# A four-layer graph network on one Trainium2 core: a lighter opening quarter of the scored sums, loads spread along it, and the first weights at the head of ScalarE's queue

## The chip, the cores and the metric

The kernel runs on one core of a Trainium2 chip. The metric is device time in microseconds (us), the lower the better. Times are medians of repeated executions; a profile is one further execution, recorded by the hardware profiler.

## What is computed

A batch of 16 graphs with 1024 nodes and 256 features passes four layers over one adjacency matrix `adj` (1024 x 1024, few of its entries not zero). Cut to what matters:

```python
# layer 0: every edge (u, v) has a score from both ends
pre_u = h @ W1[:256];  pre_v = h @ W1[256:]
S   = sigmoid(relu(pre_u[:, :, None] + pre_v[:, None, :] + b1) @ W2 + b2)
a_t = einsum('buv,bud->bvd', S * adj, h)          # the scored sums
m_t = einsum('uv,bud->bvd', adj, h) * h           # needs no score
x   = beta1 * h + beta2 * (a_t @ Wa + ba) + beta3 * (m_t @ Wm + bm)
# layer 1
x = x + relu((adj @ x) @ W.T + b)
# layers 2 and 3, softmax attention with exp(adj) as a factor
f = x @ W1.T;  f1 = f @ W2 + b2
x = softmax(leaky_relu(f1[:, :, None] + f1[:, None, :]) + adj) @ f + bias2 + x
```

## The kernel before

Only the edges that exist are scored. For each of 8 tiles of 128 nodes the kernel lists up to 16 neighbours per node in slots, and nodes with more get extra tiles of four slots. Four batches are worked on together as a group, so there are four groups. One **score step** treats one slot of one tile for one group: GpSimd gathers 128 rows of 4 KB (`z<-v_d`, L692), VectorE adds the other end (L802) and applies relu and the weight (L804), ScalarE sums it in four pieces (L808), and later GpSimd scatters the finished scores into a dense array in DRAM (`dense_d<-gt`, L697), of which the matrix products read whole tiles. Such a step moves 512 KB with its gather and 2 KB with its scatter. There are 608 of them. They are a side stream: `Side.along` (L864) adds, for each microsecond that the main stream yields as its own estimate, `RATE` steps, so that the order in which instructions are recorded interleaves the two. A scheduling layer then writes one instruction order for each engine, and every engine runs its own in order.

The main stream has these stages.

- **Opening** (L373 to L379). `load_h` loads the features of the first four batches. Batch 0 comes in four pieces of 256 KB, alternately on the SP queue and ScalarE's queue. `load_w1` (three transfers of 256 KB: both halves of W1, then Wa) follows on ScalarE's queue. `with_beta2` (L158) scales Wa on VectorE. Then come batch 1 and the adjacency matrix `adj_sb` in eight transfers on SP. TensorE turns `h` and multiplies it with W1 and Wa, while VectorE searches each row of `adj_sb` for its neighbours (L433 to L439). A flag that these searches compute decides a branch, which every engine takes.
- **The part without scores** for all 16 batches, with the scores of group 0 and some of group 1 as side stream at `RATE[0]`. Its results go to `zb_d` in DRAM.
- **Per group `with_edges`** (L1053), the scored sums: four quarters `v` of 256 columns. In each quarter, eight tiles `ut` of the dense scores are loaded on SP (`gd`, 512 KB, `load_gd`, four buffers), rearranged by ScalarE (`gc`, L1061) and multiplied on TensorE into all eight PSUM banks. At the quarter's end VectorE adds each bank to the loaded `z` (L1084), which frees the bank. The `z` of four batches (1 MB each, from `zb_d`) are loaded by `load_z`. For group 0 alone, these four loads are issued from inside the first quarter, and so are the loads of the transposed adjacency over `adj_sb` (eight of 512 KB), with an exponential by ScalarE for each (L1051).
- **Per group `pair_layers`**, twice: layers 1 to 3 for two batches.

`paced(ins, back)` (L117) makes an instruction wait until a matmul that lies `back` matmuls behind the newest recorded one has run; `back` is 6 if not given. VectorE's first operation of every score step is paced too. A load that is paced holds up all that stands behind it in SP's order.

Of the kernel before, what the change touches and what calls it, by code (L numbers as in the profile page):

```python
# [15 lines left out]
P = 128  # L16

GB = 4
BUFS = 2
RATE = (0.26, 0.255)  # L20
SLOTS = 32
FIRST = 16
EXTRA = SLOTS - FIRST
# [14 lines left out]
def after(tc, ins, others, kind, why):  # L38
    dep = mybir.DependencyInfo(kind, mybir.DependencyReason.DATA)
    for o in others:  # L40
        tc.add_manual_dep(ins.ins, o.ins.name, dep, reason=why)
# [23 lines left out]
def gnn_stack_kernel(  # L65
# [27 lines left out]
    nc = tc.nc  # L93
# [13 lines left out]
    def bank():  # L107
        return psum[-1].tile([P, HN], F32, tag="bank", name="bank")
# [8 lines left out]
    def paced(ins, back=6):  # L117


        if recent:  # L120
            after(tc, ins, [recent[max(0, len(recent) - back)]], mybir.DependencyClass.Sync, "keeps pace")
        return ins

    def product(*args, **kw):
        recent.append(nc.tensor.matmul(*args, **kw))  # L125
        del recent[:-BACK]
        return recent[-1]
# [22 lines left out]
    def load_w1(pool, queue):  # L150

        w = pool.tile([P, DH, 3, D], F32, name="w1")
        for s, a in enumerate((g0_W1[:D], g0_W1[D:], g0_Wa)):
            queue.dma_start(w[:, :, s, :], a.rearrange("(c p) k -> p c k", p=P))
        return w

    def with_beta2(w):
        return nc.vector.tensor_scalar(w[:, :, 2, :], w[:, :, 2, :], beta2, None, ALU.mult)  # L158
# [108 lines left out]
        flat = dense[i][:DUMP].rearrange("(c p r) b -> c p (r b)", p=P, r=ZERO // GB)  # L267
        return [flat[c] for c in range(flat.shape[0])]

    def load_h(pool, b, pieces=1, other=nc.sync):  # L270
        h = pool.tile([P, NT, D], F32, tag="wide", name="h")
        n = NT // pieces
        for t in range(0, NT, n):
            queue = other if t // n % 2 else nc.sync
            queue.dma_start(h[:, t : t + n, :], x[b, t * P : (t + n) * P].rearrange("(t p) d -> p t d", p=P))
        return h

    def node_pairs(t):
# [2 lines left out]
    def load_kept(pools, b):  # L281
        h = load_h(pools[0], b)
        hT = node_pairs(pools[0].tile([P, DH * N], F32, tag="wide", name="hT"))
        nc.sync.dma_start(hT.rearrange("p h n -> p (h n)"), hT_d[b])
        return h, hT
# [74 lines left out]
    with ExitStack() as stack:  # L360
        prep = stack.enter_context(tc.tile_pool(name="prep", bufs=4))
        prep1 = stack.enter_context(tc.tile_pool(name="prep1", bufs=1))
        early = stack.enter_context(tc.tile_pool(name="early", bufs=8))
        psum_pool(stack, "psum", 8)

        def first_group():
            for b in range(GB):
# [2 lines left out]
                yield 2.4  # L370
                yield from edge_sides(prep, b, w1, hT)

        hs = [load_h(early, 0, pieces=4, other=nc.scalar)]  # L373
        w1 = load_w1(prep1, nc.scalar)
        with_beta2(w1)
        hs.append(load_h(early, 1))
        for t in range(NT):
            nc.sync.dma_start(adj_sb[:, t, :], adj_v[:, t, :])
        hs += [load_h(early, b) for b in range(2, GB)]  # L379
# [292 lines left out]
    with tc.If(listed > 0) as arm:  # L672
        with ExitStack() as stack:
# [206 lines left out]
            def load_gd(g, v, ut, **pace):  # L880
                view = dense[g % BUFS][:DUMP].rearrange("(t p v) b -> t p v b", p=P, v=N)
                gd = gd_pool.tile([P, QN, GB], F32, tag="gd", name="gd")
                ins = nc.sync.dma_start(gd, view[ut][:, v * QN : (v + 1) * QN, :])
                put[g].before(paced(ins, **pace))
                return gd
# [16 lines left out]
            z_loads = []  # L902

            with ExitStack() as first:
# [12 lines left out]
                def score_free():  # L917
                    yield from turn_adj(
                        lambda n: wide_z.tile([P, DH * N], F32, tag="wide", name="stage")
                    )  # L920
                    h, hT = next_up
                    for b in range(B):
                        if b == 1:
                            nat = load_naturals(stage)
                            w1 = load_w1(own1, nc.sync)
                        if b == 2:
                            paced(with_beta2(w1))
                        if b >= GB:
                            yield from edge_sides(st_pool, b, w1, hT)
                        if b == B - 1:  # L930
                            first_hw.extend(load_hw(i) for i in range(GB - 1))
                            first_gd.extend(load_gd(0, 0, ut) for ut in range(4))
                        mT = yield from messages(pools, h, hT)
                        now = hT

                        if b + 1 < GB:
                            h, hT = load_kept(pools, b + 1)
                        elif b + 1 < B:
                            h = load_h(pools[0], b + 1)
                            hT = turned(pools[0], h)  # L940
                            yield 2.4
                        yield from without_edges(pools, b, now, mT, wm)
                        if b == 1:
                            prepare(nat)
                            yield 3

                def with_zeros(main):
                    for n, us in enumerate(main):
                        if 7 < n < 40 or n > 40 and n % 3 == 0:
                            clear()  # L950
                        yield us

                side.along(with_zeros(score_free()), RATE[0])
                assert not zeros
# [9 lines left out]
            to_load, to_exp = list(range(NT)), []  # L964
# [85 lines left out]
            def exponential(jt):  # L1050
                paced(nc.scalar.activation(ea[:, jt, :], ea[:, jt, :], AF.Exp), 16)  # L1051

            def with_edges(g, hw, z):  # L1053

                for v in range(N // QN):
                    cols = slice(v * QN, (v + 1) * QN)
                    acc = [[bank() for _ in range(DH)] for _ in range(GB)]
                    for ut in range(NT):
                        gd = first_gd.pop(0) if first_gd else load_gd(g, v, ut, back=BACK)
                        gc = gc_pool.tile([P, GB, QN], F32, tag="gc", name="gc")  # L1060
                        paced(nc.scalar.activation(gc, gd.rearrange("p n i -> p i n"), AF.Copy), 16)  # L1061
                        for i in range(GB):
                            for eh in range(DH):
                                product(
                                    acc[i][eh][:, :QN], hw[i][:, ut, eh * P : (eh + 1) * P], gc[:, i, :],
                                    start=ut == 0, stop=ut == NT - 1,
                                )
                        if z_loads and ut > 1:
                            load, i = z_loads.pop(0)
                            paced(load(i))  # L1070
                        if (to_load or to_exp) and ut % 2 and not z_loads:
                            if v and to_exp:
                                exponential(to_exp.pop(0))
                            if to_load:
                                jt = to_load.pop(0)
                                paced(nc.sync.dma_start(ea[:, jt, :], adjT_d[jt]), 16)
                                to_exp.append(jt)
                        yield 3.4
                    if v == N // QN - 1:
                        while to_exp:  # L1080
                            exponential(to_exp.pop(0))
                    for i in range(GB):
                        for eh in range(DH):
                            nc.vector.scalar_tensor_tensor(  # L1084
                                z[i][:, eh, cols], acc[i][eh][:, :QN], zbias[:, eh : eh + 1], z[i][:, eh, cols],
                                ALU.add, ALU.add,
                            )
# [109 lines left out]
            def ahead(g):  # L1197
                if g < NGR:
                    loaded.append(([load_hw(g * GB + i) for i in range(GB)], load_z(g)))
                    for load, i in z_loads:  # L1200
                        load(i)
                    z_loads.clear()

            for g in range(NGR):
                hw, z = loaded.pop(0)
                while g not in finished:
                    next(side.steps)
                side.along(with_edges(g, hw, z), RATE[1])
                side.along(pair_layers(g * GB, z[:2], lambda: None), RATE[1])
                side.along(pair_layers(g * GB + 2, z[2:], lambda: ahead(g + 1)), RATE[1])  # L1210
            assert next(side.steps, "end") == "end"
            psum.pop()

    with arm.Else():
        with ExitStack() as stack:
# [88 lines left out]
            with tc.For_i(0, B, 1) as b:  # L1304
                h = load_h(wide, b)
# [36 lines left out]
```

## Time and profile before

| | us |
|---|---|
| median of three executions (3267.03, 3267.06, 3274.82) | 3267.06 |
| the profiled execution, its own time | 3256.96 |
| its span on the core | 3255.1 |
| TensorE busy in the span | 3157.5 (97%) |
| VectorE busy | 2342.4 (72%) |
| ScalarE busy | 1879.1 (58%) |
| GpSimd busy | 1665.6 (51%) |

The mean granted TensorE clock of the profiled execution is 0.992 of full speed. All positions in the text are microseconds from the start of its span. Engine names in the views: PE is TensorE's matmuls, PEld its weight loads, DVE is VectorE, ACT ScalarE, POOL GpSimd, SP SyncE; SPq, ACTq and POOLq are what these sequencers issue. A matmul of 32-bit values is recorded as two passes.

### The profile page before, as it was taken

Reading aid. Unit: us, or ns where it says so; the run is one execution under the profiler, and the core shown is the slowest. Engines: PE = TensorE matmul, PEld = TensorE weight load, DVE = VectorE, ACT = ScalarE, POOL = GpSimd, SP = SyncE. Lnnn points to the kernel's source line nnn. Section 1 sums busy time; section 2 is a strip of 40 time slices with the busy share of each in tenths; the row PEclk is TensorE's granted clock in tenths of the full one; section 3 lists DMA queues with packets and bytes.
Section 4 is the critical chain, followed back from the end, with each engine's and each line's share of the span. In section 5 each row is a group of like instructions: output and inputs, shape, how many; then the busy total and the mean of one; then the engine's idle time right before and its main releaser. Section 6 shows DMA issues by size and latency. Waiting matters only on the chain. (4 is left out here: it accounts for less than half of the span.)

```text
span 3255.1 us, 38756 instructions
## 1 busy us (share of the span) xinstructions
PE 3157.5 (97%) x12162; PEld 2206.3 (68%) x12162; DVE 2342.4 (72%) x3217; ACT 1879.1 (58%) x6316; POOL 1665.6 (51%) x1338
## 2 busy tenths in 40 slices
PE   8899999999997999999999999999999999999999
PEld 5444545545456678578776867778686788778688
DVE  7787767777774799789678979877898881035154
ACT  3245556655667766566886656688666555322132
POOL 1156887686764666657566666665676650000000
PEclk9999999999998999999999999999999999999999
DMA  8998888878798755656875575597656635210100
GB/s 304 327 325 299 281 281 273 273 212 269 242 327 311 219 162 163 203 154 204 292 230 174 154 221 151 183 297 229 180 150 210 186 105 167 84 35 14 55 1 27
DMA packets 268438, 648.91 MB, mean 199 GB/s; under 512 B 42864, under 2 KB 131952, under 8 KB 261056
## 3 DMA queue, kind: packets, MB, share of 16 engines
q0 software_dynamic: 116704, 350.04, 36.8%
q1 hardware_dynamic: 123536, 244.66, 21.8%
q10 hardware_dynamic: 27984, 51.65, 4.2%
q8 instruction: 97, 1.59, 0.2%
q14 instruction: 117, 0.96, 0.1%
HBM read 518.84 MB, written 127.39 MB: 199 GB/s over the span
## 5 line engine op out<-in xcount | busy, mean ns | idle before, releaser
L808 ACT ACTIVATE z<-z 128x256 f32<-128x256 f32 x2432 | 979.7, 406 | 707.3 <-DVE z L804 678.2
L802 DVE TENSOR_TENSOR z<-z,u 128x1024 f32<-128x1024 f32 x608 | 738.8, 1220 | 408.2 <-PE bank L125 276.2
L125 PE MATMUL bank<-feats,m 128*128 128x257 f32 x4096 | 922.1, 383 | 20.8 <-DVE m L1033 18.7
L692 POOL DMA_INDIRECT z<-v_d,slot_v x512 | 645.9, 1262 | 463.8 <-ACT z L808 227.7
L125 PEld LDWEIGHTS bank<-feats,m 128*128 128x128 f32 x4096 | 766.3, 191 | 148.6 <-DVE m L1033 28.6
L804 DVE SCALAR_TENSOR_TENSOR z<-z,w2r 128x1024 f32<-128x1024 f32 x608 | 737.3, 1219 | 8.5
L697 POOL DMA_INDIRECT dense_d<-gt,slot_at x512 | 639.2, 1249 | 197.9 <-issue 134.7
L125 PE MATMUL bank<-gc,hw 128*128 128x256 f32 x2048 | 455.6, 384 | 30.5 <-ACT gc L1061 27.7
L808 ACT ACTIVATION_READ_ACCUMULATOR z<-z 128x1 f32 x2432 | 461.2, 190 | 0.0
L125 PEld LDWEIGHTS bank<-gc,hw 128*128 128x128 f32 x2048 | 387.2, 191 | 98.2 <-ACT gc L1061 40.4
L1033 DVE SCALAR_TENSOR_TENSOR m<-rho,tau,adj_sb 128x512 f32<-128x512 f32 x512 | 374.0, 743 | 107.7 <-PE bank L125 105.1
L125 PE MATMUL bank<-adj_sb,h 128*128 128x512 f32 x1024 | 442.4, 592 | 2.2 <-ACT st L318 2.1
L125 PE MATMUL bank<-adjT_in,y 128*128 128x512 f32 x1024 | 441.3, 592 | 1.4 <-DMA adjT_in<-adjT_d 1.4
L125 PEld LDWEIGHTS bank<-adjT_in,y 128*128 128x128 f32 x1024 | 194.4, 190 | 243.6 <-issue 228.6
L125 PEld LDWEIGHTS bank<-adj_sb,h 128*128 128x128 f32 x1024 | 194.4, 190 | 242.2 <-issue 237.7
L125 PE MATMUL bank<-w,hT 128*128 128x512 f32 (+1 forms) x1024 | 335.8, 488 | 6.8 <-DMA w<-in_L_gnn_W_dram 6.5
L1061 ACT ACTIVATE gc<-gd 128x1024 f32<-128x1024 f32 x128 | 265.5, 2074 | 88.2 <-PE bank L125 60.0
L125 PEld LDWEIGHTS bank<-w,hT 128*128 128x128 f32 x1024 | 195.0, 191 | 150.6 <-issue 126.3
L125 PE MATMUL bank<-g_wT,z 128*128 128x257 f32 x1024 | 232.9, 382 | 0.2 <-ACT st L1171 0.2
L692 POOL DMA_INDIRECT z<-v_d,x_node x96 | 127.1, 1324 | 181.8 <-ACT z L808 118.0
L125 PEld LDWEIGHTS bank<-g_wT,z 128*128 128x128 f32 x1024 | 192.9, 191 | 30.9 <-issue 3.8
L1123 DVE TENSOR_TENSOR z<-z,r 128x512 f32<-128x512 f32 x64 | 42.5, 689 | 135.2 <-ACT r L1122 134.9
(150 smaller groups left out, 2183.4 us busy)
## 6 DMA issues: line engine op xcount, KB each, us to landing
gd<-dense_d SPq DMA_DIRECT2D x128, 512.0 KB, 5.0
dense_d<-zero ACTq DMA_DIRECT2D x64, 512.0 KB, 5.9
adjT_in<-adjT_d SPq DMA_DIRECT2D x128, 256.0 KB, 3.3
h<-in_x_dram SPq DMA_DIRECT2D x19, 1024.0 KB, 12.9
u_d<-st SPq DMA_DIRECT2D x64, 256.0 KB, 5.7
v_d<-st SPq DMA_DIRECT2D x64, 256.0 KB, 6.5
hw_d<-st SPq DMA_DIRECT2D x64, 256.0 KB, 6.5
u<-u_d POOLq DMA_DIRECT2D x32, 512.0 KB, 8.1
```

The source lines that it names most:

```text
L125: recent.append(nc.tensor.matmul(*args, **kw))
L692: return nc.gpsimd.indirect_dma_start(out=dst, out_offset=None, in_=src[:], in_offset=bass.IndirectOffsetOnAxis(ap=at, axis=0), **how,)
L697: return nc.gpsimd.indirect_dma_start(out=dst[:], out_offset=bass.IndirectOffsetOnAxis(ap=at, axis=0), in_=src, in_offset=None,)
L802: paced(nc.vector.tensor_tensor(z, z, u, ALU.add))
L804: nc.vector.scalar_tensor_tensor(zk, zk, 0.0, w2r[:, None, :].to_broadcast([P, GB, D]), ALU.max, ALU.mult)
L808: nc.scalar.activation(zk[:, c, :], zk[:, c, :], AF.Copy, accum_out=s[:, k, c : c + 1])
L1033: nc.vector.scalar_tensor_tensor(m, r[:, cols], ta[:, jt : jt + 1], ea[:, jt, cols], ALU.max, ALU.mult)
L1061: paced(nc.scalar.activation(gc, gd.rearrange("p n i -> p i n"), AF.Copy), 16)
L1123: nc.vector.tensor_tensor(z[i][:, eh, cols], z[i][:, eh, cols], r, ALU.add)
```

## The change

- `RATE[1]`, the side stream's rate in `with_edges` and `pair_layers`, goes from 0.255 to 0.258.
- Opening: `load_w1` is issued first on ScalarE's queue, and all four pieces of batch 0 stand on SP's queue, ahead of batch 1. `with_beta2` is recorded after the loads of batches 0 and 1.
- Group 0, first quarter: the four `z` loads are recorded at tiles 0, 2, 4 and 6 instead of 2, 3, 4 and 5, and each is paced 12 matmuls back instead of 6. The adjacency loads begin in the second quarter instead of the first, and their exponentials in the third instead of the second. The quarter's tiles yield 1 instead of 3.4, so that the side stream gets 8 x 1 x 0.258 = 2.1 steps there instead of 8 x 3.4 x 0.255 = 6.9.

```diff
-RATE = (0.26, 0.255)
+RATE = (0.26, 0.258)
...
-    def load_h(pool, b, pieces=1, other=nc.sync):
+    def load_h(pool, b, pieces=1):
...
-            queue = other if t // n % 2 else nc.sync
-            queue.dma_start(h[:, t : t + n, :], x[b, t * P : (t + n) * P].rearrange("(t p) d -> p t d", p=P))
+            nc.sync.dma_start(h[:, t : t + n, :], x[b, t * P : (t + n) * P].rearrange("(t p) d -> p t d", p=P))
...
-        hs = [load_h(early, 0, pieces=4, other=nc.scalar)]
         w1 = load_w1(prep1, nc.scalar)
+        hs = [load_h(early, b, pieces=1 if b else 4) for b in range(2)]
         with_beta2(w1)
-        hs.append(load_h(early, 1))
...
-                        if z_loads and ut > 1:
+                        if z_loads and ut % 2 == 0:
                             load, i = z_loads.pop(0)
-                            paced(load(i))
-                        if (to_load or to_exp) and ut % 2 and not z_loads:
-                            if v and to_exp:
+                            paced(load(i), 12)
+                        if (to_load or to_exp) and ut % 2 and v:
+                            if v > 1 and to_exp:
                                 exponential(to_exp.pop(0))
...
-                        yield 3.4
+                        yield 3.4 if g or v else 1
```

## The prediction

> **What bounds the kernel now.** I read the busy row first, then TensorE's waits, then the two places that the edits touch. The page's first line gives the engine that can set the time:
>
> ```profile
> PE 3157.5 (97%) x12162; PEld 2206.3 (68%) x12162; DVE 2342.4 (72%) x3217; ACT 1879.1 (58%) x6316; POOL 1665.6 (51%) x1338
> ```
>
> TensorE is busy 97% of 3255.1 us, so 97.6 us is all that removing waits can bring. The waits of TensorE, longest in sum first, say which:
>
> ```profile
> PE bank L125 <- ACT gc L1061: 27.7, 16, 15.5
> PE bank L125 <- DVE m L1033: 18.7, 20, 2.4
> ...
> PE bank L125 <- DMA w<-in_L_gnn_W_dram: 6.5, 1, 6.5
> ```
>
> Columns: total us, times, longest. The 15.5 us piece and the 6.5 us piece belong to the two places edited. The first, in the timeline around group 0's first quarter:
>
> ```profile
> 961.49 0.32 SPq L883 DMA_DIRECT2D gd<-dense_d  x1
> ...
> 964.94 0.32 SPq L883 DMA_DIRECT2D gd<-dense_d  x1
> 965.81 3.77 SPq L897 DMA_DIRECT2D z<-zb_d  x2
> ...
> 972.24 0.32 SPq L1076 DMA_DIRECT2D adj_sb<-adjT_d  x1
> ...
> 973.10 3.92 SPq L897 DMA_DIRECT2D z<-zb_d  x2
> ...
> 977.11 1.35 SPq L883 DMA_DIRECT2D gd<-dense_d  x3
> ...
> 992.25 4.15 ACT L1061 ACTIVATE gc<-gd 128x1024 f32<-128x1024 f32 x2 [14.01 <-DMA gd<-dense_d]
> ```
>
> Columns: start, duration, engine, line, operation. The score tiles six and seven are issued only at 977.11, behind four `z` loads of 1 MB and one adjacency load, and the first of them reaches ScalarE 15 us later. The quarter in stretches:
>
> ```profile
> core 0: us, PE busy (x) PEld busy (x) DVE busy (x) ACT busy (x) POOL busy (x), PEclk, DMA share, GB/s
> 957.40:994.30 36.90, 21.30 (x97) 17.88 (x95) 13.80 (x15) 20.89 (x55) 24.21 (x20) 0.83 1.01 373
> 994.30:1001.40 7.10, 7.08 (x23) 5.88 (x24) 3.16 (x4) 3.63 (x9) 0.00 (x0) 0.68 0.48 164
> 1001.40:1094.60 93.20, 88.44 (x395) 73.14 (x394) 63.81 (x76) 91.28 (x206) 56.17 (x44) 1.00 0.86 285
> 1558.10:1672.90 114.80, 111.78 (x511) 95.40 (x510) 81.12 (x95) 108.48 (x261) 67.06 (x60) 1.00 0.85 280
> ```
>
> Until 994.3 the DMA engines are full (1.01) at 373 GB/s: this quarter is bound by DMA. The last three quarters (third row) are bound by ScalarE, busy 91.28 of 93.2. The fourth row is all four quarters of group 1, 114.8 us, of which TensorE needs 32 x 3.56 = 114: its timeline has 96 passes in 21.41 us from 957.41, and a tile takes 16 of them.
>
> **First quarter: minus 14.** DMA queues in the trace moved from 957.4 to 994.3: SP's 9.15 MB, GpSimd's 4.6 MB. Afterwards SP still owes all four `z` and five score tiles by the quarter's end, but not the adjacency tile: 9.15 - 0.5 = 8.65 MB. GpSimd's part falls with the score steps. The rate says five steps fewer; the instruction order of the built program has ScalarE do 6 steps between the quarter's first and last tile instead of 9, so 3 to 5 gathers of 0.52 MB go: 1.9 to 3.0 MB are left. At 373 GB/s, 10.6 to 11.7 MB take 28.3 to 31.2 us, beside 28.5 us of TensorE (8 tiles x 3.56). The order matters as much as the sum. In the built program the SP queue now alternates: the first `z` waits for a matmul five before the quarter, the others for the 14th, 30th and 46th, and between them come tiles four to nine. Tile six follows two `z` instead of four and is issued about 969 instead of 977.11. In the old queue 1 MB landed in about 3.4 us; counted so, tile six lands near 975.5, tile seven near 981 and the last `z` near 986.7, against TensorE's wish for 977, 980 and 986. So I expect the quarter to last 30 us instead of 44.0: -14. The ends: -9, if GpSimd keeps its bytes and 13.25 MB take 35 us; -15.5, if nothing but TensorE's 28.5 is left.
>
> The trace's clock adds to this: 0.68 after the wait against 1.00 in a running stretch. The Trainium skill, "TensorE: Matmul & The Clock Gate", Part 1, says the array returns to full speed after about 3.4 us of work; an estimate from that page is 1.7 us lost, where the row gives 7.1 x 0.32 = 2.3 us. Both lie inside the 44.0, and nothing is added for them.
>
> **Last three quarters: minus 1.** All eight exponentials (1.05 us each) remain, moved by one quarter. ScalarE's work per quarter is 8 tiles x 2.08 = 16.6, plus 1.6 per step (four sums at 0.40) and 1.05 for each `u` or exponential. Before, by the old program's order: 16.6 + 6 x 1.6 + 4.2 = 30.4, then 33.3, then 29.9, together 93.6, which the measured 93.2 confirms. After: 28.4 (TensorE 28.5 with little slack: 29), 30.4, and up to its last tile 32.3, together 91.7. That is -1.5; I take -1, with -4 and +3 as ends, because waits between the engines are not in such sums. Adjacency loads move on SP from the first quarter into a stretch with a DMA share of 0.86: 1 MB more there at 285 GB/s, covered; uncovered 2.7 us, inside the +3.
>
> **Opening: minus 1.** What is shown:
>
> ```profile
> 14.56 3.75 PE L125 MATMUL bank<-w,hT 128*128 128x512 f32 x4 [6.54 <-DMA w<-in_L_gnn_W_dram]
> 18.05 0.49 DVE L158 TENSOR_SCALAR w<-w,beta 128x512 f32<-128x512 f32 x1 [18.05 <-DMA w<-in_L_gnn_Wa_dram]
> ...
> 18.63 1.22 DVE L433 TENSOR_SCALAR_CACHE_REDUCE left<-adj_sb 128x1024 f32<-128x1024 f32 x1
> ```
>
> W's first two transfers will be where batch 0's pieces on ScalarE's queue were, and those landed, by the trace's completion counts, at 4.56 and 6.00. The third and fourth pieces of `h` come later on SP, between 8 and 10.5 instead of 5.6 to 6.0, so the sixteen turns end later too, and the first product starts at 9.5 to 11.5 instead of 14.56. These 3 to 5 us are not on the path. From 18.63 to 95.06 VectorE has no gap at all, and TensorE's small products with `full` and `missed` wait for it:
>
> ```profile
> 94.91 0.15 DVE L471 SCALAR_TENSOR_TENSOR missed<-counts,missed 128x1 f32<-128x1 f32 x1
> ...
> 95.21 0.35 PE L473 MATMUL bank<-missed,ones 128*128 128x1 f32 x2
> 95.42 10.57 PE L125 MATMUL bank<-w,hT 128*128 128x512 f32 x32
> ```
>
> TensorE gets there just when VectorE is ready. Starting earlier, it waits 3 to 4 us here. Only an earlier start of VectorE counts, and that needs the first adjacency tile, which in the trace landed at 18.61, 0.07 after `with_beta2`. On each DMA engine the same 3.25 MB stand ahead of or in this tile, in whichever queue. The DMA engines have slack in the first 20 us (share 0.82), so it may come 3 us earlier; GpSimd's small transfers may also take the share that ScalarE's queue gives up and delay it 2 us. I take -1; ends -3 and +2.
>
> Here a rule speaks against the edit. The Trainium skill, "DMA: Bandwidth & Descriptors", Issuing engines are not separate DMA queues, says that transfers of all issuing engines interleave on the same 16 DMA engines, and that issuing from several saves issue time only. By it the opening is worth 0; by TensorE's wait alone it would be -6.5.
>
> **The rest: plus 1.** The steps saved come back in `pair_layers`: by the built order 112, 113 and 102 beside groups 0 to 2 instead of 111, 111 and 101. Each brings one gather on GpSimd's queue, two VectorE operations (2 x 1.22), four on ScalarE and a scatter. VectorE is busy 87.5% there, and TensorE idles 36.9 us beside 323 steps, 0.11 us a step: four steps cost 0.5 so, or 9.8 with all VectorE time exposed. I take +1. The scheduler also reorders small pieces (turns of `feats`, `top`, `val`) there; the waits that this shuffles are 1 to 2.4 us each, one 5.9, and I allow 6 either way.
>
> Sum: -14 - 1 - 1 + 1 = -15, from 3256.96 to 3242. The median of the runs shown is 10.1 above the profiled execution; carried over, 3267.06 - 15 = 3252.
>
> **Rivals.**
>
> *A: the stall only moves (no change).* SP is in order, and each paced `z` now stands between score tiles. If the quarter stays DMA-bound at 35 us (-9) and the denser stream gives back its exposed price, with the opening at its bad end (+2), little is left: -9 + 3 + 2 + 1 = -3, or 3264; with 9.8 in place of the 1, +6, or 3273. For it: 13.25 MB stay if GpSimd's gathers run ahead. Against: the built order takes steps out of the quarter.
>
> *B: slower, through VectorE in `pair_layers`.* In order behind a late gather, VectorE once delayed TensorE:
>
> ```profile
> PE bank L1004 <- DVE top L992: 7.0, 2, 5.9
> ```
>
> Twelve fronts in groups 0 to 2 have this `top` step, and a denser stream can put it behind a gather. With five fronts at 5.9, 29.5 is lost: 3267 - 15 + 29.5 = 3282; with all twelve, 3323. From three fronts on the gain is gone, from five it is slower. Against: the rate is only 1.2% denser, and in the built order `top` has as much other work ahead of it as before.
>
> *C: the whole opening counts too.* If the adjacency tile lands by 12 us, TensorE's 5 us arrive: 3248. Against: the bytes ahead of it.
>
> **How the numbers follow.** A measurement of this kernel tells about 0.3%, or 9.8 us, from no change. The forecast (gain 11 to 19): 0.53; C: 0.09; A: 0.28; B: 0.10. C, and the forecast with it, are faster: 0.62. A is within the bound, 0.29 with a little of B; slower 0.09. From the forecast's bounds (-19.5 to -11) I go down to 3246, and up to 3270, into A; what is left out is B, the top of A and the bottom of C.
>
> **What would show it.** Right: in the first quarter TensorE's longest wait for `gc` falls from 15.5 to below 3, SP issues `z` and `gd` by turns, and the quarter ends about 30 us after it begins; TensorE's first product starts near 10.5 and a wait of 3 to 4 us for VectorE appears near 91 to 95; the sum of waits in `pair_layers` stays near 37. Wrong: a wait for `gd` above 5 us in that quarter, a first VectorE search before 15 or after 20.7, or a `pair_layers` stretch more than 6 us longer.

## The result, and the profile after

The changed kernel took 3286.2 us (median of 8 executions, 3279.9 to 3289.1), the kernel before 3272.6 (8 executions in turn with them on the same chip): ratio 1.0046, 95% interval 1.0030 to 1.0061. That is 13.6 us slower, where 15 us faster was forecast. Run again in another call (e5 below) it was 1.0018 [1.0007, 1.0029]: slower there too, by less. The profiled execution after took 3288.8 us (span 3286.8).

The busy row of the changed kernel's page:

```profile
PE 3171.8 (97%) x12162; PEld 2214.1 (67%) x12162; DVE 2344.2 (71%) x3217; ACT 1880.8 (57%) x6316; POOL 1671.1 (51%) x1338
```

The work is the same. TensorE idles more, 3286.8 - 3171.8 = 115.0 us against 97.6 before, and it is also busy longer with the same products: 3171.8 us against 3157.5. The granted clock makes most of that second part: its mean was 0.989 here and 0.992 before, and as an estimate 1.1% of 3286.8 us is 36 us and 0.8% of 3255.1 us is 26. The clock fell around waits. VectorE kept TensorE waiting for 8.3 us until 1409.7; in the rows below, with the columns of the prediction's rows of stretches, the clock is 0.50, then 1.00:

```profile
1405.30:1415.50 10.20, 5.77 (x14) 4.64 (x15) 6.13 (x12) 3.96 (x14) 6.71 (x6) 0.50 0.86 296
1415.50:1425.50 10.00, 9.96 (x45) 7.93 (x44) 8.63 (x13) 6.09 (x24) 2.42 (x2) 1.00 0.25 74
```

At the lower clock products are slower: in the opening, the 32 products behind two short waits took 13.27 us at a mean clock of 0.79, and 10.57 us at 1.00 before. So a wait can cost more than its own length. The waits of TensorE after (total us, times, longest):

```profile
PE bank L125 <- DVE m L1031: 34.0, 23, 6.6
PE bank L125 <- ACT gc L1059: 24.5, 16, 4.2
PE bank L1002 <- DVE top L990: 8.3, 1, 8.3
```

The 15.5 us piece of `gc` and the 6.5 us wait for W are gone, as meant. Yet the sum of the `gc` waits fell only from 27.7 to 24.5, and those for `m` and `top` rose, from 18.7 and 7.0 to 34.0 and 8.3, one piece of 6.6 and one of 8.3 among them. The line numbers are 2 lower than before (L1031 is L1033 of before).

**The two places that the change edits do what the prediction says.** SP's issues in group 0's first quarter (timeline after):

```profile
963.53 0.32 SPq L881 DMA_DIRECT2D gd<-dense_d  x1
965.26 0.32 SPq L895 DMA_DIRECT2D z<-zb_d  x1
966.99 0.32 SPq L881 DMA_DIRECT2D gd<-dense_d  x1
...
970.44 0.32 SPq L881 DMA_DIRECT2D gd<-dense_d  x1
972.17 0.32 SPq L895 DMA_DIRECT2D z<-zb_d  x1
```

`z` and `gd` alternate, and TensorE's longest wait in that quarter is 2.13 us:

```profile
975.56 3.72 PE L125 MATMUL bank<-gc,hw 128*128 128x256 f32 x16 [2.13 <-ACT gc L1059]
981.34 29.58 PE L125 MATMUL bank<-gc,hw 128*128 128x256 f32 x128 [2.06 <-ACT gc L1059]
```

From TensorE's first to its 129th scored pass the quarter took 34.3 us (32.0 in e5) against 46.2 counted the same way before: -11.9 to -14.2, where -14 was forecast. In the opening, TensorE starts with W sooner and then waits for VectorE's search, which starts no earlier (18.97 against 18.63):

```profile
18.97 1.22 DVE L431 TENSOR_SCALAR_CACHE_REDUCE left<-adj_sb 128x1024 f32<-128x1024 f32 x1 [9.24 <-DMA adj_sb<-in_adj_dram]
...
93.46 0.38 PE L451 MATMUL bank<-full,below 128*128 128x32 f32 x2 [1.13 <-DVE full L448]
...
95.55 0.56 PE L471 MATMUL bank<-missed,ones 128*128 128x1 f32 x2 [1.48 <-DVE total L473]
```

**The loss lies later.** The span cut at TensorE's first scored product of each group and at the end of each group's scores, in us of one profile each:

| kernel | ahead of scores | scores 0 | pairs 0, scores 1 | pairs 1, scores 2 | pairs 2, scores 3 | pairs 3 | all from scores 0 on |
|---|---|---|---|---|---|---|---|
| before | 957.4 | 137.2 | 578.3 | 579.1 | 560.2 | 443.0 | 2297.7 |
| after | 959.2 | 127.5 | 588.1 | 597.5 | 570.7 | 443.8 | 2327.6 |
| after again (e5) | 957.2 | 124.9 | 585.8 | 586.9 | 562.7 | 442.7 | 2302.9 |

The part ahead of the scores is no help here: kernels with the old opening and the same `RATE[0]` showed 950.6 to 966.6. The last column is, so what follows goes by it and by the timed ratios. The first profile after has 24.7 us more in it than e5's of the same kernel; single stalls that e5 has not (a few us near 2240 among them) make part of that, and TensorE is busy 10.4 us longer in it (2240.3 against 2229.9); the rest was not traced. Common to both is a gain in the scores of group 0, and a larger loss beside the layers of groups 0 and 1, the place of the term "the rest: plus 1".

### The profile page after: what moved, and what is told of

Same layout as the page of the kernel before. It is cut to its first block, busy times and chain, and to the rows that moved or that the text cites. A ratio compares the mean times of both kernels' runs of the same rounds, so it can differ in the third digit from the quotient of the medians.

```text
span 3286.8 us, 38765 instructions
## 1 busy us (share of the span) xinstructions
PE 3171.8 (97%) x12162; PEld 2214.1 (67%) x12162; DVE 2344.2 (71%) x3217; ACT 1880.8 (57%) x6316; POOL 1671.1 (51%) x1338
## 4 chain that ended last, share of the span: by engine, by line
PE 44%; DVE 5%; ACT 2%; issue 1%; DMA 1%; another core or an unknown queue 0%; POOL 0%; DVEq 0%; SPq 0%; ACTq 0%
PE bank L125 42%; DVE z L800 2%; DVE z L802 1%; DVE m L1031 1%; ACT z L806 1%; PE bank L1139 1%; DMA gd<-dense_d 1%; PE bank L1163 1%; ACT gc L1059 1%; PE bank L997 1%; DVE feats L135 0%; DMA dense_d<-gt,x_at 0%; DVE rho L1006 0%; DMA dense_d<-gt,slot_at 0%
## 5 line engine op out<-in xcount | busy, mean ns | idle before, releaser
L806 ACT ACTIVATE z<-z 128x256 f32<-128x256 f32 x2432 | 979.4, 405 | 676.5 <-DVE z L802 585.7
L690 POOL DMA_INDIRECT z<-v_d,slot_v x512 | 642.5, 1255 | 497.5 <-ACT z L806 277.8
L695 POOL DMA_INDIRECT dense_d<-gt,slot_at x512 | 640.4, 1251 | 195.2 <-issue 139.1
L125 PE MATMUL bank<-gc,hw 128*128 128x256 f32 x2048 | 463.3, 388 | 31.9 <-ACT gc L1059 24.5
L806 ACT ACTIVATION_READ_ACCUMULATOR z<-z 128x1 f32 x2432 | 459.8, 189 | 0.0
L1031 DVE SCALAR_TENSOR_TENSOR m<-rho,tau,adj_sb 128x512 f32<-128x512 f32 x512 | 374.4, 744 | 107.0 <-PE bank L125 105.3
L690 POOL DMA_INDIRECT z<-v_d,x_node x96 | 135.1, 1408 | 173.6 <-ACT z L806 82.6
L1082 DVE SCALAR_TENSOR_TENSOR z<-bank,zbias,z 128x256 f32<-128x256 f32 x128 | 55.4, 478 | 120.2 <-PE bank L125 119.9
```

The source lines that it names most:

```text
L690: return nc.gpsimd.indirect_dma_start(out=dst, out_offset=None, in_=src[:], in_offset=bass.IndirectOffsetOnAxis(ap=at, axis=0), **how,)
L695: return nc.gpsimd.indirect_dma_start(out=dst[:], out_offset=bass.IndirectOffsetOnAxis(ap=at, axis=0), in_=src, in_offset=None,)
L806: nc.scalar.activation(zk[:, c, :], zk[:, c, :], AF.Copy, accum_out=s[:, k, c : c + 1])
L1031: nc.vector.scalar_tensor_tensor(m, r[:, cols], ta[:, jt : jt + 1], ea[:, jt, cols], ALU.max, ALU.mult)
L1082: nc.vector.scalar_tensor_tensor(z[i][:, eh, cols], acc[i][eh][:, :QN], zbias[:, eh : eh + 1], z[i][:, eh, cols], ALU.add, ALU.add,)
```

## The experiments

Times are medians; each call ran on a chip of its own with the kernel before beside it, so only differences and ratios within a call are compared. "Scored part" is the last column of the table above.

| run | median, before in its call | difference | ratio [95%] | scored part |
|---|---|---|---|---|
| e1 opening alone | 3253.4, 3252.5 | +0.9 | 1.0001 [0.9991, 1.0011] | 2296.1 |
| e2 rate 0.258 alone | 3273.9, 3252.5 | +21.4 | 1.0062 [1.0045, 1.0078] | 2315.2 |
| e3 loads spread alone | 3248.2, 3252.5 | -4.3 | 0.9989 [0.9974, 1.0003] | 2290.9 |
| e4 lighter quarter alone | 3253.9, 3252.5 | +1.4 | 1.0006 [0.9992, 1.0020] | 2294.6 |
| e5 after again | 3259.7, 3251.9 | +7.9 | 1.0018 [1.0007, 1.0029] | 2302.9 |
| e6 after, rate 0.255 | 3249.2, 3251.9 | -2.7 | 0.9993 [0.9982, 1.0003] | 2290.1 |
| e7 before, no burst | 3239.9, 3251.9 | -12.0 | 0.9957 [0.9941, 0.9974] | 2284.0 |
| e8 after, no burst | 3242.1, 3251.9 | -9.8 | 0.9968 [0.9954, 0.9981] | 2287.7 |
| e9 rate 0.252 alone | 3269.3, 3251.7 | +17.7 | 1.0050 [1.0034, 1.0065] | 2314.6 |
| e10 rate 0.262 alone | 3274.2, 3251.7 | +22.6 | 1.0061 [1.0044, 1.0078] | 2318.7 |
| e11 after, 0.255, no burst | 3236.9, 3251.7 | -14.8 | 0.9955 [0.9939, 0.9971] | 2279.0 |
| e13 after, last `z` load later | 3257.4, 3251.7 | +5.8 | 1.0016 [1.0007, 1.0026] | 2307.0 |
| e14 rate 0.258, no burst | 3257.4, 3259.8 | -2.4 | 0.9992 [0.9978, 1.0006] | 2301.7 |
| e15 rate 0.252, no burst | 3260.6, 3259.8 | +0.8 | 0.9997 [0.9980, 1.0014] | 2302.7 |
| e16 rate 0.262, no burst | 3264.5, 3259.8 | +4.7 | 1.0015 [1.0000, 1.0030] | 2311.0 |
| e17 after, rate 0.252 | 3270.3, 3259.8 | +10.5 | 1.0026 [1.0013, 1.0040] | 2310.7 |

### Which part of the change costs

Each of the four edits was put alone into the kernel before.

**e1**, the opening alone:

```diff
-        hs = [load_h(early, 0, pieces=4, other=nc.scalar)]
         w1 = load_w1(prep1, nc.scalar)
+        hs = [load_h(early, b, pieces=1 if b else 4) for b in range(2)]
         with_beta2(w1)
-        hs.append(load_h(early, 1))
```

> Only the opening is changed: W first on ScalarE's queue, all four pieces of batch 0 on SP. Theory R (the denser side stream is what costs: the rate of 0.258 brings the score steps back where VectorE and GpSimd have no room): the opening costs about 3 us, as it does in the changed kernel (109.7 against 106.5 us to the first turn of the adjacency matrix), and nothing after it moves: +3 us. Theory O (any edit that shifts the side stream against the main stream deals anew where its bursts meet the main chain, whatever the rate): the same +3, since no step is shifted. Theory T (the opening delays what follows by more than its own 3 us, because the clearing of the dense arrays and the stores start later): +8 or more.

Ratio 1.0001: nothing, within 3.6 us. VectorE's search bounds the opening, and it starts when the adjacency tile lands. In single profiles TensorE came to its first turn of the adjacency matrix even later than before (106.5): at 108.0 in e1 and 109.7 after. Between 94 and 110 its mean clock was 0.89 and 0.79 there, against 1.00 from 94 to 106.5 before; the interval is too wide to show this in the time.

**e2**, the constant alone:

```diff
-RATE = (0.26, 0.255)
+RATE = (0.26, 0.258)
```

> Only the rate goes from 0.255 to 0.258. Theory R: the whole of the loss behind group 0's scored sums comes from here, so groups 1 and 2 take 15 to 20 us each more or half of it, and the total is 15 to 30 us above the kernel before, with the first quarter's 15 us wait unchanged. Theory O: the steps are dealt anew, and the total lies anywhere from -10 to +25, with TensorE's waits in other places than in the changed kernel. Theory T: no change.

Plus 21.4 us, more than the whole change costs. This is the part of the change that the prediction had wrong.

**e3**, the `z` and adjacency loads and the exponentials spread, nothing else:

```diff
-                        if z_loads and ut > 1:
+                        if z_loads and ut % 2 == 0:
...
-                            paced(load(i))
-                        if (to_load or to_exp) and ut % 2 and not z_loads:
-                            if v and to_exp:
+                            paced(load(i), 12)
+                        if (to_load or to_exp) and ut % 2 and v:
+                            if v > 1 and to_exp:
```

> Only the z loads and the adjacency loads with their exponentials are spread as in the changed kernel; rate and yields are as before. Theories R and T: group 0's scored sums fall by 5 to 9 us of the 9.7 that the changed kernel gained there, since the score tiles no longer stand behind four z loads, and the rest stays: -5 to -9 us. Theory O: the same in the scored sums, and the rest within 5 us of before, since the recorded steps are not shifted.

The scores of group 0 take 130.0 us instead of 137.2, and the time falls by 4.3 us with an interval that just holds zero.

**e4**, the lighter quarter alone:

```diff
-                        yield 3.4
+                        yield 3.4 if g or v else 1
```

> Only the first quarter of group 0 yields 1 instead of 3.4 per tile, with the rate at 0.255. About five score steps leave that quarter and come later. Theory R: the first quarter falls by 3 to 6 us since GpSimd's queue moves 2.5 MB less, nothing is denser later, the side stream merely ends 20 us of main work later, inside group 2: -3 to -6 us. Theory O: all later steps are shifted by five against the main stream, as the changed kernel shifts them, so groups 1 and 2 lose what they lose there: +10 or more.

The scores of group 0 take 131.9 us, 5.3 less, but the steps saved there are dealt to later places (575.0, 581.0 and 563.7 us in the next three columns, against 578.3, 579.1 and 560.2), and the time does not fall. In the last of these columns TensorE waits 3.12 us because the last group's scores come later (e17 below shows this at its largest).

**e5 and e6** are the changed kernel once more, and the changed kernel with the constant back:

```diff
-RATE = (0.26, 0.258)
+RATE = (0.26, 0.255)
```

> The changed kernel itself, on the same chip as the next three. The rate alone cost 20 us, the spread loads gained 4, the opening and the lighter yields did nothing measurable. Theory A (the parts add): +14 to +18. Theory O (every combination deals the steps anew): anywhere from 0 to +25.

> The changed kernel with the rate put back to 0.255, everything else changed. Theory A: without the rate's 20 us the rest is worth 4 to 9 us, so -4 to -9 against the kernel before, and group 0's scored sums keep the 9.7 us they gained. Theory O: the loss stays in part, 0 to +15, since the lighter quarter alone already shifts all later steps.

The constant is worth 10.5 us in the changed kernel (3259.7 against 3249.2). Without it the change is a gain of 2.7 us that its interval does not tell from nothing, although its scored part is 7.6 us shorter in the profile.

### What the constant does: a burst of scatters

When a group's last score step is recorded, all its waiting scatters are issued at once. They stand on GpSimd's queue ahead of the next group's gathers. GpSimd in e2:

```profile
1391.43 0.97 POOL L697 DMA_INDIRECT dense_d<-gt,slot_at  x1 [0.30 <-issue]
1392.71 0.97 POOL L697 DMA_INDIRECT dense_d<-gt,slot_at  x1 [0.30 <-DMA dense_d<-gt,slot_at]
1393.98 0.98 POOL L692 DMA_INDIRECT z<-v_d,slot_v  x1 [0.30 <-issue]
```

Sixteen scatters run so without a gather from 1370.61 to 1393.7, 23 us or 1.4 each. VectorE, then TensorE, in the same place:

```profile
1400.35 1.23 DVE L802 TENSOR_TENSOR z<-z,u 128x1024 f32<-128x1024 f32 x1 [12.63 <-DMA z<-v_d,slot_v]
```

```profile
1403.49 1.23 PE L125 MATMUL bank<-g_wT,z 128*128 128x257 f32 x2 [7.09 <-DVE z L1123]
```

VectorE runs in order and is held for 12.63 us by the step whose gather is late. Behind it stands L1123, which adds layer 1's result to `z`, and TensorE needs that `z` for the next product: 7.09 us are lost. Before, the same sixteen scatters, from 1373.85 on, hold VectorE for 4.15 us until 1401.76, after L1123 has run, and TensorE loses 2.16 and 1.11 (in this fence and the next two the first line is VectorE's):

```profile
1401.76 1.23 DVE L802 TENSOR_TENSOR z<-z,u 128x1024 f32<-128x1024 f32 x1 [4.15 <-DMA z<-v_d,slot_v]
1403.38 0.43 PE L999 MATMUL bank<-ident,feats 128*128 128x128 f32 x2 [2.16 <-DVE feats L135]
1404.91 0.46 PE L1004 MATMUL bank<-ident,top 128*128 128x128 f32 x1 [1.11 <-DVE top L992]
```

So the burst is in both kernels, and the constant moves it against the main stream. Group 2 has such a burst too. Before, it cost TensorE 5.86 us:

```profile
2046.69 1.23 DVE L802 TENSOR_TENSOR z<-z,u 128x1024 f32<-128x1024 f32 x1 [6.85 <-DMA z<-v_d,slot_v]
2048.05 0.47 PE L1004 MATMUL bank<-ident,top 128*128 128x128 f32 x1 [5.86 <-DVE top L992]
```

After, VectorE waited 9.13 us and TensorE 6.59:

```profile
2061.03 1.23 DVE L800 TENSOR_TENSOR z<-z,u 128x1024 f32<-128x1024 f32 x1 [9.13 <-DMA z<-v_d,slot_v]
2062.97 9.43 PE L125 MATMUL bank<-feats,m 128*128 128x257 f32 x32 [6.59 <-DVE m L1031]
```

Both bursts together made TensorE wait 9.1 us before (2.16, 1.11 and 5.86) and 14.9 after (8.29 for `top` at 1409.7, and 6.59).

**e7 and e8** take the burst away, from the kernel before and from the changed one: the last scatters are issued one or two a step like all others, and the group counts as finished when none of them is left. That holds for groups 0 to 2; the last group's scatters, seventeen in a row, still go at once.

```diff
 if t == last_of[g]:
-    for group, *what in waiting:
-        group.add(scatter(*what))
-    waiting.clear()
-    finished.append(g)
+    if g < NGR - 1:
+        closing.append(g)
+    else:
+        ...
...
+if closing and not any(w[0] is put[closing[0]] for w in waiting):
+    finished.append(closing.pop(0))
```

> The kernel before, but a group's last scatters are no longer issued in one burst: they leave at the usual one or two a step, between the gathers of the next group. Theory B (where the burst falls against the main chain is what the rate shifts; in the traces 12 to 16 scatters stand ahead of the next gathers, and VectorE then waits 4.1 and 6.9 us in the kernel before, 12.6 and 8.1 with the rate alone): TensorE's waits around 1400 and 2045 us go, -6 to -10 us. Theory R (density alone): the two waits move elsewhere, -3 to +3.

> The changed kernel without the burst. Theory B: most of the rate's loss goes, so it stands 0 to +5 above the same edit of the kernel before, and 10 us or more below the changed kernel. Theory R: it stands 12 us or more above the same edit of the kernel before, whatever both gain.

The bursts cost 12.0 us in the kernel before and 17.6 in the changed kernel (3259.7 - 3242.1). In the profiles of before and e7 the scored part differs by 13.7 us: TensorE idles about 8 us less (63.1 against 71.0) and is busy 5.7 us less with the same products. The two kernels without bursts (3239.9 and 3242.1) differ by 2.2 us instead of 7.9, and e7's trace has no wait of VectorE for a gather above 5 us beside the layers. Yet of the 9.2 us that e8's scores of group 0 are shorter, nothing is left in its scored part, which is 3.7 longer than e7's. The burst is part of the loss and not all of it.

### Density, order, or SP's queue

**e9 and e10** are the kernel before with `RATE[1]` at 0.252 and at 0.262. **e13** is the changed kernel with one load moved, because the traces with 0.258 had the fourth `z` load of group 1 ahead of the second `gd` on SP:

```diff
-                    for load, i in z_loads:
-                        load(i)
-                    z_loads.clear()
+                    while len(z_loads) > 1:
+                        load, i = z_loads.pop(0)
+                        load(i)
...
-                        if z_loads and ut % 2 == 0:
+                        if z_loads and ut % 2 == 0 and (not g or ut >= 4):
```

> The kernel before with the rate of the score steps in the scored part at 0.252 in place of 0.255, nothing else. Three theories of why the single constant 0.258 alone cost 20 us. Theory R (density: more score steps per microsecond of TensorE's work take VectorE, ScalarE and GpSimd from that work): the time falls with the rate, so 0.252 gives up to 20 us less than before, 3232 to 3252. Theory O (order: the constant only shifts which score step falls beside which product, and with it whether a burst of scatters or a transfer falls on a sensitive place): no monotony, a time within 15 us of before on either side. Theory S (the order on SP's queue at the start of group 1, as one part of O): here three gd loads stand ahead of the last z load, as in the changed kernel at rate 0.255, so the scores of group 1 take 118 to 121 us, 2 to 4 less than before's 122.6, whatever the rest does.

> The kernel before with the rate at 0.262, twice as far up as the change goes. Theory R: about 40 us over before, 3285 to 3300, and at least over the 20 us of 0.258. Theory O: not in line with 0.258, anywhere from 3237 to 3285. Theory S: three gd loads again stand ahead of the last z load, so the scores of group 1 take 118 to 122 us although the rate is higher; R would have them at 126 or more.

> The changed kernel, rate 0.258, with one z load of each later group (the fourth, which waits until the last pair of the group before is done with its z) recorded after the fifth score tile of the group instead of ahead of the first; on SP's queue seven gd loads then stand ahead of it instead of one. Theory S (that z load holds the gd loads behind it, and TensorE waits for gc at the start of group 1): the scores of group 1 take 119 to 123 us instead of the changed kernel's 127 to 128.5, and the time is 5 to 8 us below the changed kernel's, 3252 to 3255 where that stood at 3260, near the kernel before. Rival (what makes the start of group 1 long is not SP's order but scores of the next group beside it, or the pace of 24 products that the gd loads keep): 127 to 129 us still, and a time within 2 us of the changed kernel's.

Theory R falls as it was put: a lower rate costs 17.7 us, and 0.262 hardly more than 0.258. The 17.7 lies outside the 15 us that theory O allowed as well. All three neighbours of 0.255 cost 18 to 23 us, and each in another stretch: against before, 0.252 loses 5.6 us in "pairs 0, scores 1" and 9.6 in "pairs 2, scores 3", 0.258 loses 9.6 in the first of these, 0.262 loses 12.0 in "pairs 1, scores 2". For 0.258 the stretch is that of group 1's burst. At 0.252 most of the 9.6 is something else: the last group's scores come late, and TensorE waits 5.09 us for them at 2712.8 (see e17).

Theory S falls as well, though my expectation of e9 and e10 seemed to bear it out (the scores of group 1 took 121.0 and 118.2 us there). In e13 seven `gd` loads stand ahead of that `z`, the scores of group 1 took 131.1 us, and the time is 5.8 us over before against 7.9, which the intervals do not tell apart. I had also read that stage wrongly: its length holds products of the layers before whenever TensorE's order starts the scores ahead of them, which is why the table above joins the two. What TensorE waits for there, in e5, is on ScalarE:

```profile
1544.75 2.06 ACT L1059 ACTIVATE gc<-gd 128x1024 f32<-128x1024 f32 x1 [2.19 <-DMA gd<-dense_d]
...
1551.05 1.04 ACT L844 ACTIVATE u<-b1r 128x1024 f32<-128x1024 f32 x1
...
1555.57 3.92 ACT L1059 ACTIVATE gc<-gd 128x1024 f32<-128x1024 f32 x2
```

```profile
1557.62 24.73 PE L125 MATMUL bank<-gc,hw 128*128 128x256 f32 x105 [4.20 <-ACT gc L1059]
```

Between two `gc` ScalarE is dealt the sums of three steps (L806, four to a step), one `u` and the last results of the pair, with no gap above 0.83 us; in e6 the corresponding `gc` start at 1543.10, 1549.44 and 1552.94. That reading was not tested by a run of its own.

**e14, e15 and e16** are the three rates without the bursts of groups 0 to 2 (the edits of e2, e9 and e10, each with that of e7), **e17** is the changed kernel at 0.252.

> The kernel before with the rate at 0.258 (alone plus 20 us) and with the last scatters of a group spread over the next steps instead of issued in one burst (alone minus 12.0 us, 3240). Theory B (the rate costs what it costs because the steps, dealt anew, put VectorE's search behind a burst of some 13 to 16 scatters on GpSimd at a place where TensorE has no product in stock): without a burst the rate is nearly free, 3238 to 3245. Theory O (each deal also has other costly places, with no burst in them): the rate still costs 12 to 20 us, 3252 to 3262.

> The same at the rate 0.252 (alone plus 17.7 us). Theory B: 3238 to 3245. Theory O: 3250 to 3260.

> The same at the rate 0.262 (alone plus 22.6 us). Theory B: 3238 to 3247. Theory O: 3252 to 3265.

> The changed kernel at the rate 0.252, with the burst as it was. If 0.255 is a value that happens to deal the steps well in both kernels, 0.252 costs here as 0.258 did, 5 to 18 us over the changed kernel at 0.255 (3249): 3254 to 3267. If the changed opening quarter moves the deal, so that the place of 0.255 is no longer special, 3243 to 3252, on either side.

Neither theory has it alone (their ranges were counted from 3252; the kernel before had 3259.8 in this call). Set against e7's -12.0, the rates 0.252, 0.258 and 0.262 cost 12.8, 9.6 and 16.7 us without the burst, and 17.7, 21.4 and 22.6 with it. So the bursts make 5 to 12 us of the loss and the rest remains. These are differences between calls, each ratio with an interval of about 5 us either way: the remainders of 10 to 17 are good to some 7 us, the burst's shares to some 9, so that only the 12 at 0.258 stands clear of nothing. In the changed kernel 0.255 is the best of three as well: -2.7, against +7.9 at 0.258 and +10.5 at 0.252, the last losing 22 us in "pairs 2, scores 3", where e6 has 564.7 and it has 586.7. That loss has nothing to do with gathers behind a burst. In e17:

```profile
2687.47 1.35 POOL L695 DMA_INDIRECT dense_d<-gt,slot_at  x1 [20.23 <-DVE gt L819]
...
2706.94 0.97 POOL L695 DMA_INDIRECT dense_d<-gt,slot_at  x1 [0.30 <-issue]
2709.10 7.05 SPq L881 DMA_DIRECT2D gd<-dense_d  x4
2714.58 5.79 PE L125 MATMUL bank<-gc,hw 128*128 128x256 f32 x16 [19.58 <-ACT gc L1059]
```

The loads of the last group's score tiles wait for its last scatter, and TensorE stands still for 19.58 us. The same wait is 5.09 us in e9, 4.74 in e11, 4.44 in e15, 3.13 in e6 and 3.12 in e4; in the kernel before the last scatter ended at 2677.4 and the first such load was issued at 2690.97, with room to spare. So fewer steps, by a lower rate or by the lighter quarter, have a price of their own: the side stream comes late for the last group. With the burst gone, 0.258 costs the changed kernel 5.0 (e8's -9.8 against e11's -14.8, in two calls).

GpSimd in e14 at the place shown of e2, gathers now between the scatters:

```profile
1384.12 0.98 POOL L697 DMA_INDIRECT dense_d<-gt,slot_at  x1 [0.30 <-issue]
1385.40 0.97 POOL L697 DMA_INDIRECT dense_d<-gt,slot_at  x1 [0.30 <-issue]
1386.68 1.44 POOL L692 DMA_INDIRECT z<-v_d,slot_v  x1 [0.30 <-issue]
```

What stays open is the remainder of 10 to 17 us. At 0.252 the late last group is a large part of it. At 0.258 it has no one place: in e14 against e7 the columns differ by 3.3, 6.3, 0.6 and 7.5 us, made of single waits of at most 4.2 us (from 1080 to 2760 TensorE waited 26.6 us for `m` and 10.0 for `gc`, in e7 19.0 and 7.8). Of the 17.7 us between the scored parts of these two profiles, 8.1 are idle time of TensorE and 9.6 are longer busy time (2230.5 against 2220.9).

A rival stands untested here: density, above 0.255. Without the bursts, -12.0, -2.4 and +4.7 rise in step with the rate. Each rate adds steps beside the layers, 1.2% and 2.7% of 323; as an estimate, at the prediction's 2.44 us of exposed VectorE time each, these are 9.5 and 21.6 us, and the remainders are 9.6 and 16.7. No run separates this from the place of the steps.

**e11** joins what the runs point to: the changed kernel with the rate at 0.255 and without the burst (the edits of e6 and e8).

> The changed kernel with the rate back at 0.255 and with the last scatters of a group issued a few at a time instead of in one burst. If the two gains add (2.7 us of the changed kernel at 0.255, 12.0 us of the kernel before without the burst), 3252 less 14.7, 3235 to 3240. If the order rules (theory O), each edit deals the steps anew and the sum holds only to some 10 us: 3228 to 3248. Either way below before.

3236.9 us, ratio 0.9955 [0.9939, 0.9971]: the sum of e6's -2.7 and e7's -12.0 is -14.7, measured -14.8. It is faster than the kernel before, and than the changed kernel by the ratios (0.9955 against 1.0018), but its interval overlaps that of e7, the burst's removal alone.

## Why the prediction was wrong

- **First quarter, minus 14: right.** 34.3 and 32.0 us instead of 46.2; the loads alone brought 37.6 (e3), the lighter quarter alone 41.5 (e4). The old quarter was taken as 44.0 us and is 46.2 by the count of passes. The bound named was the right one: up to 990 the DMA engines' share is 1.00 at 370 GB/s. The scores of group 0 as a whole fell by 9.7 and 12.3 us.
- **Last three quarters, minus 1.** 91.1 us before, 93.2 after and 92.9 in e5, counted from the 129th pass: plus 2, inside the end of +3. One term there was short: 1 MB at 285 GB/s takes 3.5 us, not 2.7.
- **Opening, minus 1: nothing**, 1.0001 with e1 alone. The estimate from TensorE's wait alone, -6.5, was far off. The first product came at 13.27 where about 10.5 was forecast, and the wait of 3 to 4 us for VectorE was 1.13 + 1.48 = 2.6. What the Trainium skill says ("DMA: Bandwidth & Descriptors", Issuing engines are not separate DMA queues), that transfers of all issuing engines interleave on the same 16 DMA engines, agrees with e1's 1.0001; VectorE's search began at 18.46 there and at 18.63 before.
- **The rest, plus 1: the failed step.** The constant, which this term was to pay for, was worth +10.5 us in the changed kernel (e5 against e6) and +21.4 alone (e2). By the table, everything behind the scores of group 0 took 17.5 us more in e5 than before, and 2.9 more with the constant back (e6). The step counted four more score steps at a mean price, 0.11 us each, or 2.44 each of exposed VectorE time, as though the constant changed an amount. What the runs showed in its place: the constant moves where the steps and the bursts of scatters fall, two bursts made TensorE wait 14.9 us instead of 9.1, and the burst's removal took 17.6 us from the changed kernel. Whether the rest is place or density stays open. The 6 us "either way" allowed for reordering was taken from waits in one trace, one order among many, so it could not bound what another order makes of the same queues: at group 1's burst 8.29 us (after) and 7.09 (e2), where before had 2.16 and 1.11. It also counted idle time alone, as the 97.6 us named as all that removing waits can bring: e7 shortened TensorE's busy time as well, from 3157.5 to 3151.1.
- **Rival B was the right kind and was set too low.** It named VectorE behind a late gather. Against it I held that "the rate is only 1.2% denser", an argument on the amount again. Its price, five fronts at 5.9, was wrong: the long waits for a late gather come at two bursts a run, not at many `top` steps, and `top` lost 8.3 us once. The 5.9 itself was the wait behind group 2's burst, and the 1.1 beside it in that row the one behind group 1's. That sixteen scatters stood ahead of each of these gathers was there to read in the trace of before.
- **Rival A** had the quarter stay at 35 us; it fell to 34.3 and 32.0, so the stall did go. The other half of it, a gain given back later, holds for e4 and, with e6's -2.7, perhaps for the change without the constant: the scored part gains 7.6 us in the profile, and about a third of that is seen in the time. **Rival C** falls with e1.
- **The carry-over.** The sum went onto the median shown, 3267; the kernel before measured 3272.6 beside the changed one. 5.5 us of the miss are this.

## What to carry to other kernels

Where two streams are interleaved by a rate, a small change of the rate deals every later step anew, so price it by the spread over neighbouring rates (here 18 to 23 us for 1% to 3%) and not by the count of steps. Here 0.255 beat its neighbours on both sides in both kernels; nothing shows that it would after another edit, so try again after each one that moves the deal. Ask also by when the side stream must be done: at 0.252 the last group waited for it, up to 19.58 us. A burst on an in-order queue that feeds another in-order engine is worth spreading by itself: it was 12 us in the kernel before. And price a wait of TensorE by more than its length where the clock falls around it.

## What the hardware showed that I had not expected

- The kernel before had medians of 3251.7 to 3272.6 us in five calls, four of them on known and different chips, 0.64% apart: more than the whole change costs in either call.
- Where two profiles of one kernel are undisturbed, they repeat wait by wait: in the scores of group 2, after and e5 have 3.86 and 3.92, 2.73 and 2.72, 1.41 and 1.40 us at the same products. What looks like noise between orders is fixed by the order.
- A scatter of 2 KB holds GpSimd's queue about as long as a gather of 512 KB: 1251 and 1255 ns on average in the changed kernel's profile.
